# Five moves in the instruction order of a one-core attention and gated-expert kernel: first weights, key jobs, first softmax, output weights, bias

## Chip, core and metric

The kernel runs on one core of a Trainium2 chip. The core has a matrix engine (TensorE, PE in the profile; its weight loads stand apart as PEld), a vector engine (VectorE, DVE), a scalar engine (ScalarE, ACT), a slower general engine (GpSimd, POOL) and SyncE (SP), which issues nearly all DMAs. PE writes its results to PSUM, which this kernel uses as seven accumulators of 128 x 512 floats, `acc0` to `acc6`, and one more bank, `misc`. The metric is the device time of a launch in microseconds.

## What is computed

x has 2 x 2048 tokens of 2048 features. It is normalised, and two things are added to x: an attention of one head of width 512 and a low-rank expert layer of 64 experts of rank 8.

```python
xn = layernorm(x)
q, k, v = split(xn @ Wqkv + bqkv)
attn = softmax(q @ k.T / sqrt(512)) @ v @ Wo + bo
scores = (xn @ Wq_w.T) @ keys.T
gate = softmax of the 16 largest scores, 0 elsewhere
ffn = 2 * ((xn @ A_w.T) * gate, per expert) @ B_w.T
return x + attn + ffn
```

Everything is in 32-bit floats.

## The kernel before

**Numbers.** A float is split in two: `hi`, a copy in the reduced format `fp32r` that PE takes (`split_hi`, line 127, on ScalarE), and `lo`, what is left (`split_lo`, line 130, on VectorE). A product is three matmuls, lo x hi, hi x lo and hi x hi (`PASSES`, `product`, line 135). So each operand costs a ScalarE cast and a VectorE residue before PE can use it.

**Stages.** The 4096 tokens are 8 blocks of 512.

1. `first_block` (0 to some 70 us) makes value projections of block 0 out of rows of x: four row tiles of 128 tokens are loaded (`load`), their statistics taken (`normal`: `bn_stats` on VectorE, a power on POOL), scaled (`scale`), transposed on PE (`turn`, four groups of four) and split. Weights come in eight pieces: `piece()` loads one and casts it, `low(n)` makes its residue, on POOL for pieces 2 to 4, on VectorE for the others. `ps[t]` is the accumulator of row tile t. `turn` writes its groups into banks 0, 1, 2 and 0 again; `ps` takes banks 3 to 6.
2. Blocks 0 and 1 are projected plainly. The pairs of blocks (2,3), (4,5) and (6,7) are projected by a scheme of seven products in place of eight. Its phases are P1, P2, P6, P5, P3, P7, P4, each with six feature items and one value item `V` (first in P2 and P3, last in the others). An item takes 24 matmuls of 0.227 us, 5.4 us; a value item 96 shorter ones, 11.8 us. Weight pieces (`fetch`, tiles `pw`) are loaded two items ahead, cast and split. `beside` lists what each phase does next to its products, step by step, some steps behind each item: `split_steps` for the next phase's tokens, and in the last pair *key jobs* (`key_list`) and query sums (`query_steps`). A key job reads a quarter of a block's keys, makes the seven combinations for the scores and stores them: seven casts, seven residues and four sums of 128 x 256, two loads, four stores. In the last pair, P6 has jobs 0 to 2, P5 3 and 4, P7 5 and 6, and P4 job 7 with the loads (`ql`, `kl`) and splits (`qp`) of the first queries.
3. Scores. Four pairs of query blocks against eight key groups, seven products each: 224 steps g of six matmuls, 1.36 us (`score`, line 1170). Exact row maxima are kept (`greatest`, line 1134), gathered at the end of a block (`maxes`, lines 1210 to 1222) and spread over the partitions by a matmul (`spread`, line 1232). `side` holds, by step g, what is dealt beside: `keys`, `combos` (combinations of the output weights: four loads, four sums, lines 1344 to 1347, four stores), and the first softmax. `begin[0]` is step 65, the first at which weighted sums run between the scores.
4. `soft(c, part)` makes the softmax of one unit of 128 x 1024: part 0 subtracts the maximum (line 1252), part 1 takes the exponential (line 1256), part 2 casts, splits and adds to the sum (lines 127, 130, 1268). `weigh` multiplies with the values (line 135, `acc<-ph,vt`).
5. After the last score the weighted sums of blocks 6 and 7 run alone, c = 0 to 31, with the first loads of the output projection beside them; `load_bo(0)` loads the bias for half of the output columns. Then the output projection runs in seven products again (line 1464). `residual` loads a tile of x and adds the bias to it on POOL (line 1448).

**What sets the order.** The program is one list. Each engine works through its own instructions strictly in the order in which the build puts them; the build takes them by readiness and by place in the program, so that a load can stand far ahead of where it is written. `behind(...)` pins an instruction behind a given earlier one of the same engine. A DMA on SP waits, in its place, until its target is free or its source is written, and what is behind it on SP waits too.

Of the kernel before, what the change touches and what calls it, by code (L numbers as in the profile page):

```python
# [26 lines left out]
NT = T // P  # L27
# [35 lines left out]
def attn_ffn_kernel(ctx: ExitStack, tc, x, xT, wq, wv, wob, bqk, bv, bo, keysT, out):  # L63
# [36 lines left out]
    def acc(n=None):  # L100

        if n is None:
            n = banks.pop(0)
            banks.append(n)
        return psum.tile([P, T], F32, name="acc", tag=f"acc{n}", bufs=1)
# [230 lines left out]
    def first_block():  # L336


        xs0 = [r_xs, r_xs, r_xs] + [big(j) for j in range(16, 21)]
        xn = [r_xh([P, 2, T], FR, "xh") for c in range(NCH)]  # L340
        rows, mv = {}, const.tile([P, NT, 2], F32, name="mv", bufs=2)
        rs = const.tile([P, NT], F32, name="rs")
        nm = const.tile([P, NT], F32, name="nm")

        def load(t, cols):
            rows[t] = [xs0[2 * t + c]([P, 1024], F32, "xs") for c in range(2)]
            for c in range(2):
                for h in range(1024 // cols):
                    a = h * cols
                    (nc.scalar if t == 0 and c else nc.sync).dma_start(  # L350
                        rows[t][c][:, a : a + cols],
                        x[t * P : (t + 1) * P, c * 1024 + a : c * 1024 + a + cols],
                    )

        def normal(t):
            st = const.tile([P, 4, 6], F32, name="st6", bufs=2)
            row_stats(mv[:, t, :], rows[t], 0, st)
            last["nm"] = nc.vector.tensor_scalar(nm[:, t : t + 1], mv[:, t, 0:1], -1.0, None, ALU.mult)
            rstd(rs[:, t : t + 1], mv[:, t, 1:2], 1)

        def scale(t):
            for n in range(4):
                c, h = divmod(n, 2)
                v = rows[t][c][:, h * 512 : (h + 1) * 512]
                if n < 3:
                    last["row"] = nc.vector.tensor_scalar(
                        v, v, mv[:, t, 0:1], rs[:, t : t + 1], ALU.subtract, ALU.mult
                    )
                else:
                    nc.scalar.activation(v, v, AF.Identity, bias=nm[:, t : t + 1])  # L370
                    last["mul"] = nc.scalar.mul(v, v, rs[:, t : t + 1])

        def turn(t, g0=0, g1=NCH // 4):
            sl = slice(t * P, (t + 1) * P)
            for g in range(g0, g1):
                pt = acc(g % 3)
                for j in range(4):
                    c = 4 * g + j
                    k = (c % 8) * P
                    nc.tensor.transpose(pt[:, j * P : (j + 1) * P], rows[t][c // 8][:, k : k + P], ident)  # L380
                for part in range(2):
                    for j in range(4):
                        hi, lo = (xn[4 * g + j][:, a, sl] for a in range(2))
                        pj = pt[:, j * P : (j + 1) * P]
                        if part == 0:
                            split_hi(hi, pj)
                        else:
                            last["row"] = split_lo(lo, pj, hi)

        r_w0 = Ring(sb, "h0", "h1", "h2", "h3", "B25", "B26", "B32", "B33")  # L390

        def mul(ps, wh, t, c2):
            sl = slice(t * P, (t + 1) * P)
            for cc in range(2):
                c = 2 * c2 + cc
                product(
                    ps[:, :VH], lambda a: xn[c][:, a, sl], lambda b: wh[:, b, cc, :],
                    c == 0, c == NCH - 1,
                )

        N2 = NCH // 2
        warm = half(0)([P, T], mybir.dt.bfloat16, "warm")
        nc.vector.memset(warm, 0.0)
        pw = misc()
        for j in range(25):
            nc.tensor.matmul(pw, warm[:, :P], warm, start=True, stop=True)
        load(0, 512)
        normal(0)
        scale(0)

        wh = []

        def piece():
            wh.append(wv_hi(0, len(wh), r_w0))

        def low(n):
            with behind("row", "nm", "mul"):
                wh[n] = weights_lo(*wh[n], nc.gpsimd if 2 <= n < 5 else None)

        piece()  # L420
        piece()
        low(0)
        low(1)
        piece()
        turn(0, 0, 2)
        low(2)
        piece()
        turn(0, 2, 4)
        low(3)
        piece()  # L430
        low(4)
        load(1, 1024)
        ps = [acc(3 + t) for t in range(NT)]
        with behind("row"):
            normal(1)
        piece()
        low(5)
        load(2, 1024)
        for t in range(NT):
            for c2 in range(N2):  # L440
                if t + 1 < NT and c2 == 2:
                    scale(t + 1)
                    if t + 2 < NT:
                        with behind("row"):
                            normal(t + 2)
                if t == 0 and c2 == 4:
                    for n in range(6, N2):
                        piece()
                        low(n)
                    load(3, 1024)  # L450
                    constants()
                if t + 1 < NT and c2 == 6:
                    with behind("pe"):
                        turn(t + 1)
                mul(ps[t], wh[c2], t, c2)
        qr = router_in()
        for t in range(NT):
            with behind("row"):
                values_out(0, t, 0, r_ev, qr, ps[t])
        flush()  # L460
        ps = [acc(t) for t in range(NT)]
        banks[:] = 4, 5, 6, 0, 1, 2, 3
        for c2 in range(N2):
            w = wv_piece(1, c2)
            for t in range(NT):
                mul(ps[t], w, t, c2)
        for t in range(NT):
            values_out(0, t, 1, r_ev, qr, ps[t])
        return xn, qr
# [208 lines left out]
    def mixed(*lists):  # L678

        n = max(map(len, lists))  # L680
        return [
            st for k in range(n) for ls in lists
            for st in ls[k * len(ls) // n : (k + 1) * len(ls) // n]
        ]

    def beside(j, ph):
# [34 lines left out]
        if ph == "P3":  # L721
            if more:
                n = x_steps(j + 1, *b00)
                steps = mixed(split_steps(j, "P7", *b01), n[1][:2])
                return n[0], s1[-2:-1] + steps[:3] + s1[-1:] + steps[3:]
            q_ = query_steps(0, big(*GROUPS[3]), ((0, 1),))
            return [], q_[:1] + mixed(split_steps(j, "P7", *b01), q_[1:3]) + [lambda: None] + q_[3:]
        if ph == "P7":
            if more:
                n = x_steps(j + 1, *b10)  # L730
                return n[0], mixed(split_steps(j, "P4", *b10), n[1][:2])
            ks_ = key_list(5, 7)
            q_ = query_steps(1, big(*GROUPS[2]), ((0, 1),))
            return [], q_[:1] + mixed(split_steps(j, "P4", *b10), q_[1:3], ks_[:-6]) + ks_[-6:] + q_[3:]
        if more:
            return x_steps(j + 1, *b01)[0] + x_steps(j + 1, *b11)[0], mixed(
                x_steps(j + 1, *b00)[1][2:], split_steps(j + 1, "P1", *b00)[:2],
# [3 lines left out]
        kl = lambda i: lambda: key_load(i)  # L741
        k = key_list(7, 8, False)
        return [], [
            [ql(0), ql(1)], [qp(0), ql(2), *k[:2]], [qp(1), ql(3), *k[2:4]], [qp(2), ql(4), *k[4:6]],
            [qp(3), ql(5), *k[6:]], [qp(4), ql(6), kl(0), kl(1)], [kl(2), kl(3), qp(5), qp(6)],
        ]

    XU, YU, XV, YV = {}, {}, {}, {}
# [326 lines left out]
    n = 0  # L1075
# [475 lines left out]
        keys(n, g, g - 2)  # L1551
    spaced(NG1 + 36, query_steps(2, r_tp))
    spaced(2 * NG1 + 35, query_steps(3, r_tp))
    slots = [2 * NG1 + 45, 2 * NG1 + 50] + [3 * NG1 + k for k in (9, 17, 38, 44, 50, 56)]
    for k, g in enumerate(slots):
        spaced(g, combos(k // ND, k % ND))

# [13 lines left out]
                    deal(g, [loads[n]])  # L1571
                deal(g if n < 4 else g + 4, [splits[n]])
    deal(begin[0] - 8, [lambda c=c: load_v(c) for c in range(3)])
    deal(begin[0] - 3, [lambda c=c: soft(c) for c in range(2)])
    done = 0
    last["add"] = last["dve"]
    for g in range(begin[-1]):
# [45 lines left out]
    while done < NW * NPAIR:  # L1623
        weigh(done)
        done += 1
        c, d = divmod(done - NW * (NPAIR - 1), ND)
        if d == 0 and 1 <= c <= 18:

            k, part = (c - 1) // 2, (c - 1) % 2
            if part == 0:  # L1630
                if k < 8:
                    half_of[k] = moving(0, STEPS[k // 2], 2 * (k % 2))
                    with behind("sp"):
                        half_of[k][0]()
            elif k:
                half_of[k - 1][1]()
        if d == 0 and c == 18:
            load_bo(0)
        if d == 0 and c in (20, 24, 28):
            ahead(c // 4 - 5)  # L1640
# [75 lines left out]
```

## Time and profile before

| | |
|---|---|
| time, median of 3 runs | 2615.39 us (2614.67 to 2617.12) |
| profiled execution, its own time | 2614.46 us |
| span of its trace | 2612.3 us |
| mean granted PE clock | 0.998 |
| matmuls of line 1464, output projection | 609.4 us, x2688, 389 ns |
| matmuls of the pair phases, 128 x 512 | 694.0 us, x3024, 390 ns |
| adds of the bias on POOL, line 1448 | 234.4 us, x128, 1838 ns |
| packets of the 16 DMA engines | 608.08 MB, mean 233 GB/s |

A duration is that of one instruction from start to end; neighbours overlap, so 128 x 512 matmuls of 390 ns follow each other every 227 ns. Idle time is given with what ended it. Stretches and instructions are in us from the start of the span; "x4" is four instructions put in one row, and what stands in square brackets is the idle time just before the row and who ended it.

### The profile page before, as it was taken

The numbers are of one execution on the slowest core, as the hardware profiler recorded it, in microseconds if no ns is written. First come the engines' busy times: TensorE is split into PE (matmuls) and PEld (weight loads), VectorE is DVE, ScalarE is ACT, GpSimd is POOL, SyncE is SP. The second block draws the span as 40 slices with busy tenths as digits, with TensorE's granted clock in tenths as the row PEclk, the third lists the DMA queues.
The fourth block names the chain that finished last, engine by engine and source line by source line (L and its number), as shares of the span: only waits on it lengthen the run. The fifth ranks groups of instructions, "written<-read, shape, count | busy, mean of one in ns | idle before, by whom it ended". The sixth has DMA issues, their size and how long they took to land. (4 is left out here: it accounts for less than half of the span.)

```text
span 2612.3 us, 34449 instructions
## 1 busy us (share of the span) xinstructions
PE 2588.7 (99%) x12690; PEld 2187.4 (84%) x12690; DVE 1910.3 (73%) x2688; ACT 925.1 (35%) x1377; POOL 548.2 (21%) x318
## 2 busy tenths in 40 slices
PE   8999999999999999999999999999999999999999
PEld 8889888888888888888887888878877888888887
DVE  6557639867878677776768869688698776787675
ACT  4333323323332233343445546354364222332221
POOL 2311420001000010000000000000032655576654
PEclk9999999999999999999999999999999999999999
DMA  6667775668436684577999798788898545565552
GB/s 236 241 245 259 280 268 188 207 215 278 158 129 225 220 275 130 170 259 244 314 323 317 243 338 282 270 317 282 276 325 289 170 156 164 188 213 181 170 166 101
DMA packets 326649, 608.08 MB, mean 233 GB/s; under 512 B 27672, under 2 KB 150608, under 8 KB 326480
## 3 DMA queue, kind: packets, MB, share of 16 engines
q1 hardware_dynamic: 313520, 575.99, 65.0%
q10 hardware_dynamic: 12960, 29.89, 3.4%
q8 instruction: 100, 1.64, 0.3%
q14 instruction: 69, 0.57, 0.1%
HBM read 450.42 MB, written 155.35 MB: 232 GB/s over the span
## 5 line engine op out<-in xcount | busy, mean ns | idle before, releaser
L135 PE MATMUL acc<-t,pw 128*128 128x512 f32 x3024 | 694.0, 390 | 3.7 <-DVE pw L130 3.7
L135 PEld LDWEIGHTS acc<-t,pw 128*128 128x128 f32 x3024 | 565.3, 188 | 121.9 <-DVE pw L130 4.1
L1464 PE MATMUL acc<-wb,s 128*128 128x512 f32 x2688 | 609.4, 389 | 0.0
L1464 PEld LDWEIGHTS acc<-wb,s 128*128 128x128 f32 x2688 | 504.5, 188 | 104.8
L1448 POOL TENSOR_TENSOR xo<-xo,bo_bc 128x512 f32<-128x512 f32 x128 | 234.4, 1838 | 868.8 <-DMA bo_bc<-in_bo 593.0
L135 PE MATMUL acc<-ph,vt 128*128 128x512 f32 x1536 | 380.0, 392 | 4.2 <-DVE ph L130 2.4
L135 PEld LDWEIGHTS acc<-ph,vt 128*128 128x128 f32 x1536 | 289.0, 189 | 67.7 <-DVE ph L130 3.5
L1170 PE MATMUL acc<-qt,kt 128*128 128x512 f32 x1344 | 334.2, 391 | 1.1 <-DVE qt L130 1.0
L1170 PEld LDWEIGHTS acc<-qt,kt 128*128 128x128 f32 x1344 | 252.2, 188 | 56.8 <-DVE qt L130 2.2
L127 ACT CAST pw<-pw 128x1024 fp32r<-128x1024 f32 (+1 forms) x168 | 177.7, 1058 | 343.3 <-PE acc L135 236.1
L130 DVE TENSOR_TENSOR pw<-pw 128x1024 fp32r<-128x1024 f32 (+1 forms) x168 | 213.4, 1270 | 70.9 <-ACT pw L127 69.5
L135 PE MATMUL acc<-xh,wh 128*128 128x512 f32 x1152 | 263.6, 390 | 0.0
L135 PEld LDWEIGHTS acc<-xh,wh 128*128 128x128 f32 x1152 | 215.6, 188 | 44.9
L127 ACT CAST s<-xz 128x1024 fp32r<-128x1024 f32 x112 | 118.0, 1055 | 376.3 <-PE acc L1464 314.2
L135 PEld LDWEIGHTS acc<-pw,t 128*128 128x128 f32 x2016 | 245.7, 188 | 2.0 <-DVE yv L790 0.8
L135 PE MATMUL acc<-pw,t 128*128 128x264 f32 x2016 | 246.4, 283 | 0.6 <-DVE yv L790 0.6
L130 DVE TENSOR_TENSOR s<-xz,s 128x1024 fp32r<-128x1024 f32 x112 | 170.7, 1526 | 45.3 <-ACT s L127 45.3
L130 DVE TENSOR_TENSOR wh<-wu,wh 128x512 fp32r<-128x512 f32 x96 | 82.0, 870 | 97.6 <-ACT wh L127 97.4
L544 POOL TENSOR_TENSOR zt<-zt,g 128x512 f32<-128x512 f32 x24 | 39.9, 1672 | 504.3 <-DMA g<-gd 275.7
L1453 DVE TENSOR_TENSOR xo<-xo,acc 128x512 f32<-128x512 f32 x128 | 86.8, 680 | 52.7 <-POOL xo L1494 24.1
L127 ACT CAST t<-xq 128x1024 fp32r<-128x1024 f32 x84 | 88.3, 1051 | 98.2 <-PE acc L135 41.3
L130 DVE TENSOR_TENSOR t<-xq,t 128x1024 fp32r<-128x1024 f32 x84 | 106.2, 1269 | 22.1 <-ACT t L127 21.6
(166 smaller groups left out, 2488.1 us busy)
## 6 DMA issues: line engine op xcount, KB each, us to landing
vt<-v_d SPq DMA_DIRECT2D x128, 512.0 KB, 5.8
kt<-kp_d SPq DMA_DIRECT2D x224, 256.0 KB, 5.9
pw<-sq_d SPq DMA_DIRECT2D x72, 512.0 KB, 4.2
xo<-in_x SPq DMA_DIRECT2D x128, 256.0 KB, 3.3
xz<-oz_d SPq DMA_DIRECT2D x64, 512.0 KB, 4.6
out_y<-xo SPq DMA_DIRECT2D x128, 256.0 KB, 2.5
pw<-in_wq SPq DMA_DIRECT2D x54, 512.0 KB, 4.3
wu<-in_wq SPq DMA_DIRECT2D x48, 512.0 KB, 6.1
```

The costliest lines, as they stand in the source:

```text
L127: return nc.scalar.copy(hi, src)
L130: return (eng or nc.vector).tensor_tensor(lo, src, raw(hi), ALU.subtract)
L135: last["pe"] = nc.tensor.matmul(ps, st(a_), mv(b_), start=first and n == 0, stop=end and n == 2)
L544: nc.gpsimd.tensor_tensor(zt, zt, gx[n], ALU.mult)
L1170: last["pe"] = nc.tensor.matmul(ps, st[:, d, a, :], mv[c][:, d, :], start=not more and d == 0 and i == 0, stop=d == 1 and i == 2, skip_gro ...
L1448: nc.gpsimd.tensor_tensor(xs, xs, bo_bc[q // (NB // 2 * NH), c], ALU.add)
L1453: nc.vector.tensor_tensor(xs, xs, ps, op)
L1464: nc.tensor.matmul(ps, st[a_][:, kk, sl], mv[b_], start=not more and kk == 0 and n == 0, stop=kk == ND - 1 and n == 2, skip_group_check=more,)
```

## The change

- In `turn` the four groups go to banks 0, 1, 2 and 6. `ps` is no longer taken at once: the accumulator of row tile t is taken when its products begin.
- Pieces 5, 6 and 7 are loaded and cast right behind row tile 1, ahead of row tile 2; the residue of piece 5 comes ahead of the statistics of row tile 1.
- In the last pair, job 5 goes from P7 to P3; the query sums' stores in P7 come ahead of the last five key steps. In P4 the splits of the first queries come one item later, and the steps of key job 7 are grouped 3, 2, 3.
- The `combos` slots of the last quarter go from 9, 17, 38, 44, 50, 56 to 7, 14, 21, 38, 44, 50.
- The first softmax unit is dealt in three parts at steps 60, 61 and 62, the second half of it at 63; before, both at 62 and 63.
- `load_bo(0)` is written at c = 28 in place of c = 18.

```diff
-                pt = acc(g % 3)
+                pt = acc((0, 1, 2, 6)[g])
...
         load(1, 1024)
-        ps = [acc(3 + t) for t in range(NT)]
+        for n in range(5, N2):
+            piece()
+        low(5)
         with behind("row"):
             normal(1)
-        piece()
-        low(5)
         load(2, 1024)
+        ps = []
         for t in range(NT):
+            ps.append(acc(3 + t))
             for c2 in range(N2):
...
                 if t == 0 and c2 == 4:
-                    for n in range(6, N2):
-                        piece()
-                        low(n)
+                    low(6)
+                    low(7)
                     load(3, 1024)
                     constants()
...
             q_ = query_steps(0, big(*GROUPS[3]), ((0, 1),))
-            return [], q_[:1] + mixed(split_steps(j, "P7", *b01), q_[1:3]) + [lambda: None] + q_[3:]
+            ks_ = key_list(5, 6)
+            return [], q_[:1] + mixed(split_steps(j, "P7", *b01), q_[1:3], ks_[:-5]) + q_[3:] + ks_[-5:]
...
-            ks_ = key_list(5, 7)
+            ks_ = key_list(6, 7)
             q_ = query_steps(1, big(*GROUPS[2]), ((0, 1),))
-            return [], q_[:1] + mixed(split_steps(j, "P4", *b10), q_[1:3], ks_[:-6]) + ks_[-6:] + q_[3:]
+            return [], q_[:1] + mixed(split_steps(j, "P4", *b10), q_[1:3], ks_[:-5]) + q_[3:] + ks_[-5:]
...
-            [ql(0), ql(1)], [qp(0), ql(2), *k[:2]], [qp(1), ql(3), *k[2:4]], [qp(2), ql(4), *k[4:6]],
-            [qp(3), ql(5), *k[6:]], [qp(4), ql(6), kl(0), kl(1)], [kl(2), kl(3), qp(5), qp(6)],
+            [ql(0), ql(1)], [ql(2), *k[:3]], [qp(0), ql(3), *k[3:5]], [qp(1), ql(4), *k[5:]],
+            [qp(2), qp(3), ql(5)], [qp(4), ql(6), kl(0), kl(1)], [kl(2), kl(3), qp(5), qp(6)],
...
-    slots = [2 * NG1 + 45, 2 * NG1 + 50] + [3 * NG1 + k for k in (9, 17, 38, 44, 50, 56)]
+    slots = [2 * NG1 + 45, 2 * NG1 + 50] + [3 * NG1 + k for k in (7, 14, 21, 38, 44, 50)]
...
-    deal(begin[0] - 3, [lambda c=c: soft(c) for c in range(2)])
+    deal(begin[0] - 5, [lambda c=c: soft(0, c) for c in range(3)])
+    deal(begin[0] - 2, [lambda: soft(1)])
...
-        if d == 0 and c == 18:
+        if d == 0 and c == 28:
             load_bo(0)
```

## The prediction

> **What bounds the kernel.** I read the page's engine shares first, then the list of who waited for whom, cut to TensorE (PE), then the table by stretches around each hole, and last the order of time inside it.
>
> ```profile
> span 2612.3 us, 34449 instructions
> PE 2588.7 (99%) x12690; PEld 2187.4 (84%) x12690; DVE 1910.3 (73%) x2688; ACT 925.1 (35%) x1377; POOL 548.2 (21%) x318
> ```
>
> ```profile
> PE acc L135 <- DVE wh L130: 3.8, 1, 3.8
> PE acc L135 <- DVE pw L130: 3.7, 1, 3.7
> PE misc L1232 <- DVE mq L1222: 2.5, 3, 1.2
> PE acc L135 <- DVE ph L130: 2.4, 1, 2.4
> ...
> PE acc L135 <- ACT ph L127: 1.2, 1, 1.2
> ```
>
> The waits are us in total, times, longest. PE idles 2612.3 - 2588.7 = 23.6 us, in a few holes. No matmul is added or removed, so the change is worth only what it does to holes and to the half-clock stretches behind them. Distances between matmul starts put the holes at 15.9 to 19.7 us (first weights), 1290.2 to 1294.1 (last phase, P4, of the last pair), 1412.8 to 1415.1 (first softmax), 1899.4 to 1900.6 (last maxima) and 1988.9 to 1991.5 (end of the weighted sum). Each edit touches one of them.
>
> ```profile
> 1288.89:1292.30 3.41, 1.48 (x7) 1.00 1.01 394
> 1292.30:1295.71 3.41, 1.63 (x7) 1.00 0.90 363
> 1411.77:1415.18 3.41, 1.57 (x7) 1.00 0.95 303
> 1415.18:1418.59 3.41, 3.41 (x8) 0.50 0.27 92
> ...
> 1988.62:1992.03 3.41, 1.00 (x5) 1.00 0.63 186
> 1992.03:1995.44 3.41, 3.41 (x9) 0.50 0.45 161
> ```
>
> The columns are the stretch, its length, PE busy, granted clock, DMA share, GB/s. Twice here, and again at 19.13 to 22.54, PE ran for 3.41 us at half clock, which costs up to 3.41 / 2 = 1.7 us. **Row against rule.** The Trainium skill, "TensorE: Matmul & The Clock Gate" ("HAM oscillation"), puts the limit at idle gaps of over about 3.4 us. In this trace holes of 0.65 and 1.19 us together, and one of 2.6, were followed by half clock, while the hole of 3.9 us, split over two windows with 1.48 and 1.63 busy, was not. The rows fit a count of work per window: 1.00 busy, or 1.57 of which 0.47 is one matmul of only 48 rows, is too little; 1.48 of full ones is enough. By the rule, closing the 1413 and 1990 holes would save the holes alone; by the row 1.7 us more each, 3.4 in all. I take the row.
>
> **1. First weights.** Nothing is added. Pieces 6 and 7 (2 x 270 KB) now go ahead of row tile 2 (1 MB) on SP, which then lands about 0.54 MB / 0.37 MB per us = 1.5 us later; its statistics ran at 21.5, behind work that ends no earlier than 20.6 (below), so that is hidden.
>
> ```profile
> 15.23 0.88 DVE L130 TENSOR_TENSOR xh<-acc,xh 128x128 fp32r<-128x128 f32 x4 [1.68 <-ACT xh L127]
> 16.03 2.46 DVE L206 BATCH_NORM_STATS2 st<-xs 128x6 f32<-128x512 f32 x4
> ```
>
> VectorE (DVE) sets this stage. Four banks for the transposes take away its 1.68 us wait, so its first residues end near 14.3 instead of 16.1. Then comes the residue of piece 5 (0.70, from 14.5, when ScalarE has cast it), then the statistics (2.46 + 0.27 + 0.2, to 18.2), then POOL's power (0.96), which the piece used to hide and which now lies bare. Scaling of row tile 1 starts near 19.2 instead of 20.1. PE does piece 5 at about 15.5 to 16.2 and then waits for the transposes of that tile, at 19.8 instead of 20.97: the hole moves, and the slow window stays. Gain 1.1. Against it: bank 6 is also the accumulator of row tile 3, whose first matmul must now wait for the sixteenth residue of its own transposes. In the old trace these ran 38.4 (first transpose) to 43.1 (last residue), with 16 x 0.11 + 12 x 0.12 = 3.2 us of PE work to cover 4.7: 1.5 lost, where PE ran on before. Net loss 0.4 (from 2 gained to 3.3 lost, if that hole also brings a slow window).
>
> **2. Key jobs.** One job (7 casts of 0.41 on ScalarE; 7 residues and 4 sums of 0.42 on DVE = 4.6 us; 2 loads and 4 stores on SP) goes from P7 to P3. DVE was busy 8.88 and 8.21 of 10 us in 1204 to 1224 (P3), and 9.70 and 8.16 in 1254 to 1274 (P7). Also the query splits of P4 come an item later.
>
> ```profile
> 1284.78 0.80 SPq L631 DMA_DIRECT2D pw<-in_wq  x1
> ...
> 1290.22 1.04 ACT L127 CAST qt<-qt 128x1024 fp32r<-128x1024 f32 x1 [3.28 <-DMA qt<-qs_d]
> 1291.72 1.04 ACT L127 CAST pw<-pw 128x1024 fp32r<-128x1024 f32 x1 [0.46 <-DMA pw<-in_wq]
> ```
>
> The weight piece was issued only at 1284.78: on SP it stands behind the value stores of P7 (1277.5 to 1283.5), which wait for a DVE that was late with key steps. It landed 6.9 us later, in a stretch with the DMA at 0.95 to 1.03. With 4.6 us less on DVE I put the stores 3.5 us earlier, so the piece near 1281.3, landing 1288.2, cast 1289.3, residue 1290.5, no longer behind a query cast: needed at 1290.2, hole 0.3 to 0.5. Gain 3.4 (nothing if only ScalarE's order changes, since the landing alone explains 1291.64; 3.9 at most; a loss is the second rival).
>
> **3. First softmax.** The subtraction stood at 1411.52 on DVE, behind both sums (1409.11 and 1409.92). Dealt two steps earlier it follows the first: 1409.8, exponential 1411.2, cast 1412.3 to 1413.0 instead of 1414.47 to 1415.09. PE's 1.19 us and 0.13 for the residue go. The 0.65 before the maxima product stays, since the same DVE work is ahead of it; it is what is late next. With 1.2 more busy the window keeps full clock: 1.7. Gain 3.0 (0 to 3.6).
>
> **4. Output weights.** The eighth combination job leaves slot 56 of the last quarter. Its four sums (0.69 each) at 1891.73, 1892.94, 1894.56 and 1897.04 stood inside the chain of the last maxima, whose end at 1900.48 held PE 1.38 us. Gain 1.4 (0 to 1.5). The other slots move by up to three steps: the load at 175 may wait on SP for stores of `ot` (landed about 1758), some 2 us ahead of key loads that are issued eight steps (11 us) early. Hidden; DVE at 3.62 and 5.46 of 10 in 1810 to 1830 takes the job at 189.
>
> **5. The bias.**
>
> ```profile
> 1988.75 2.15 POOL L1448 TENSOR_TENSOR xo<-xo,bo_bc 128x512 f32<-128x512 f32 x1 [0.66 <-DVE L L1268]
> 1989.70 1.75 DVE L130 TENSOR_TENSOR ph<-sp,ph 128x512 fp32r<-128x512 f32 x1
> ```
>
> Five POOL adds in 1971 to 1991 each lengthen one DVE operation by 1.1 us (0.68 to 1.79, 1.22 to 2.31), 5.4 in all, and PE waits 2.57 for the last residue. Whether the edit moves an add is not sure: the load of the bias stands at 1902.43 in the trace, far ahead of its place in the program (near 1956), so the build orders it by readiness. But the DMAs of the eighth combination leave SP between 1886 and 1898, where token loads may go instead, and part 4 frees DVE time. I take one add less before the last residue: 1.1 + 1.7 (busy 2.1 in that window) = 2.8, between 0 and 2.6 + 1.7 = 4.3.
>
> **Sum.** +0.4 - 3.4 - 3.0 - 1.4 - 2.8 = -10.2 on the profiled execution's 2614.46 (span plus 2.2): 2604.3. The median of the three runs is 0.9 above it: 2605.2.
>
> **Rivals.** *Half of it*: the DMA still sets the landing of the P4 piece and the bias moves nothing, the case in which two parts don't do what they say. +0.4 - 3.0 - 1.4 = -4.0: 2611.4. For it: DMA at 0.95 and the bias at 1902. Against: SP's queue is visibly late.
>
> *Slower*: the key job in P3.
>
> ```profile
> ACT kst L127 <- DMA kp_d<-kst: 33.4, 19, 5.1
> ```
>
> ScalarE waited 19 times for a key store to land, 1.8 us on average, 5.1 at most, with weight casts queued behind it. P3's fifth item has 1.4 us of slack (residue ends 1217.4, needed about 1218.8). Each of the four new stores can cost 5.1 - 1.4 = 3.7; from the third on it eats the whole gain. Four: 14.8, and two slow windows 3.4, so 18.2 - 10.2 = 8.0 lost: 2623.4. Against it: the average wait is near the slack, and P5 carries two jobs with no hole.
>
> *All of it*: 1.1 without the bank wait, 3.9, 3.0, 1.4, 4.3, and the small waits at 1951 and 1964 (0.6 + 0.3): -14.6, 2600.8.
>
> **Chances.** Forecast 0.50, half 0.22, slower 0.13, all 0.15. A measurement of this kernel can tell about 0.2% (5.2 us) from no change. Faster: 0.50 + 0.15 + 0.03 of the half case = 0.68; the rest of that case and a little of the third make no change 0.20, slower 0.12. Range 2600.0 to 2617.5: it takes in the first, the half and the full case and part of the slower one.
>
> **What would show it.** Half clock gone after 1415 and 1992, still there near 19 to 23; PE waiting near 41 us for a residue of `xh`; the P4 piece issued on SP by about 1281 and no PE wait on `pw`; no wait of 1.2 us before the last `mq` product; fewer lengthened DVE operations before the last `ph`. It is wrong if a PE wait on `pw` appears in P3 or P7, or if the bank wait at 41 us brings a slow window.

## The result and the profile after

The changed kernel takes 2608.03 us (median of 8 runs, 2605.63 to 2610.36) against 2615.89 us for the kernel before (8 runs, 2611.67 to 2619.87). The ratio is 0.9971, 95% interval 0.9960 to 0.9982, so 7.9 us are gained (4.7 to 10.5). The forecast was 2605.2, in a range of 2600.0 to 2617.5. The total was near. What it is made of was not: of its five steps one came out at its place in the size worked out and one roughly, two brought nothing at their place, one had its gain by way of another edit, and an amount of 3.3 us was in no sum.

First the page of the changed kernel, then its list of who PE waited for (us in total, times, longest):

```profile
span 2608.6 us, 34456 instructions
PE 2587.2 (99%) x12690; PEld 2186.9 (84%) x12690; DVE 1910.3 (73%) x2688; ACT 924.8 (35%) x1377; POOL 520.0 (20%) x318
```

```profile
PE acc L135 <- DVE xh L130: 3.7, 3, 1.5
PE acc L380 <- DVE xs L366: 3.2, 2, 3.0
...
PE acc L1172 <- ACT sp L1182: 1.5, 1, 1.5
```

PE idles 2608.6 - 2587.2 = 21.4 us where it idled 23.6. The waits of 3.7 for `pw`, of 3.8 for `wh` and of 2.4 for `ph` are gone or small. In their place stand 3.0 for the scaled row tile (`xs`), 1.4 for the bank of row tile 3 (one of the three waits for `xh`; the longest of them, 1.5, is for residues of row tile 1), 1.5 for ScalarE's copy of `sp`, and (not copied here) 1.8 for `yv`, in a part of the kernel that no edit touches. (From line 433 on, line numbers of the changed kernel are one to three higher than before.)

This profiled execution is the slowest of its eight, 2610.36 us, only 4.1 below the profiled one of before, while the medians differ by 7.9. Two profiles alone would mislead here, and the reason for it is the main finding. The same stretches as in the prediction (length, PE, PEld, DVE, ACT and POOL busy, granted clock, DMA share, GB/s), of the changed kernel:

```profile
1291.24:1294.66 3.42, 3.42 (x16) 2.82 (x15) 0.83 (x3) 0.57 (x2) 0.00 (x0) 1.00 1.03 311
1410.83:1414.25 3.42, 1.88 (x8) 0.84 (x6) 3.36 (x8) 2.05 (x3) 0.00 (x0) 1.00 1.03 335
1414.25:1417.66 3.41, 3.41 (x9) 2.73 (x9) 2.43 (x4) 2.28 (x5) 0.00 (x0) 0.50 0.05 17
```

The hole at 1290 is closed: PE is busy throughout, as it is from 1987 to 1994 (3.40 of 3.40 us in two stretches), in the place of the hole at the end of the weighted sum. The one at 1413 is not closed, and half clock follows it as before.

### The profile page after: what moved, and what is told of

Same layout as the page of the kernel before. It is cut to its first block, busy times and chain, and to the rows that moved or that the text cites. A ratio compares the mean times of both kernels' runs of the same rounds, so it can differ in the third digit from the quotient of the medians.

```text
span 2608.6 us, 34456 instructions
## 1 busy us (share of the span) xinstructions
PE 2587.2 (99%) x12690; PEld 2186.9 (84%) x12690; DVE 1910.3 (73%) x2688; ACT 924.8 (35%) x1377; POOL 520.0 (20%) x318
## 5 line engine op out<-in xcount | busy, mean ns | idle before, releaser
L1450 POOL TENSOR_TENSOR xo<-xo,bo_bc 128x512 f32<-128x512 f32 x128 | 207.4, 1627 | 893.2 <-DMA bo_bc<-in_bo 588.8
```

What stands on the lines that cost most here:

```text
L1450: nc.gpsimd.tensor_tensor(xs, xs, bo_bc[q // (NB // 2 * NH), c], ALU.add)
```

## The experiments

Each kernel was run beside the kernel before; a ratio is to that, with its 95% interval, and 0.1% is 2.6 us. Every run also reports its mean granted clock, to three digits. One minus it, times the span, is the time that half clock can cost, half of what its stretches last (it costs less where PE would wait anyway); its mean over many runs tells more than one profile. For the kernel before it is 0.9971 over 91 runs, 7.6 us.

**The five edits one by one.** The first takes only the first weights:

```diff
-                pt = acc(g % 3)
+                pt = acc((0, 1, 2, 6)[g])
...
-        piece()
-        low(5)
...
+        ps = []
```

> The kernel before with the first edit alone (banks 0, 1, 2, 6 for the transposes, pieces 5 to 7 ahead of row tile 2, residue of piece 5 ahead of the statistics). Theory 'by the trace after': this edit is a loss of about 2 us: PE stands for row tile 3's first product (1.4 us, bank 6), has nothing of row tile 0 left to put beside the transposes, and keeps its hole of 3 us at 17 to 20. Time 2616 to 2619, +0.05 to +0.15%. Theory 'by the prediction': +0.4 us, so nothing that can be told, and the stage ends near where it did. Rival 'window': if the loss seen in the profile is only another phase of the half-clock window, the stage ends within 0.5 us of before's (event at 82 us).

Measured: 0.9998 (0.9989 to 1.0006), nothing that can be told. The first stage ends when PE starts its first 128 x 512 product. With this edit that is at 72.80, 71.75 (the changed kernel, two profiles) and 71.33 us (this run), mean 72.0; in eight profiles without the edit it is at 70.70 to 72.02, mean 71.1. The ranges overlap, so a cost of some 0.8 us is an estimate from few profiles; it lies between the two theories.

The reverse, the changed kernel with this edit undone:

> The changed kernel with the first edit undone. By the trace after: 2 us faster than the changed kernel, near 2606, 0.9963 of before. By the prediction: 0.4 us faster, 0.997. If edit 1 had gained at its place (-1.1 without the bank wait): slower than the changed kernel by 1 us, 0.9975.

Measured: 0.9964 (0.9951 to 0.9976), in the direction of the first theory, but the interval holds the changed kernel's 0.9971 too, and at its very end the 0.9975 of a gain at its place. The time does not decide.

The slots of the combination jobs alone (`slots`, last quarter: 7, 14, 21, 38, 44, 50):

> The kernel before with the new slots of the combination jobs alone; the bias load stays written at c = 18. By the trace after: the freed places on SP around 1890 take four token loads and the bias, four POOL adds run before 1912, the hole at 1990 and the half clock behind it go (-4.3), the 1.4 us before the last maxima go but a wait of 1.5 us for a tile comes at 1892: -4 us in all, 2612. By the prediction (parts 4 and 5 gain each at its own place): -1.4, hole at 1990 still there with the load of the bias left where it was: 2614.5.

Measured: 0.9984 (0.9977 to 0.9990), -4.2 us, as the first theory has it. The bias load is left where it was written, and yet the hole at 1990 is gone. POOL's timeline (start, us) of this run shows why:

```profile
1907.17 6.66 POOL L1448 TENSOR_TENSOR xo<-xo,bo_bc 128x512 f32<-128x512 f32 x4 [591.17 <-DMA bo_bc<-in_bo]
```

PE ran without a wait through the place of the hole:

```profile
1974.66 23.28 PE L135 MATMUL acc<-ph,vt 128*128 128x512 f32 x102
```

Four adds now run in a row at 1907, in 1.7 us each. In the profile of before only one stood there, and took 21.35 us:

```profile
1907.63 21.35 POOL L1448 TENSOR_TENSOR xo<-xo,bo_bc 128x512 f32<-128x512 f32 x1 [593.01 <-DMA bo_bc<-in_bo]
```

Five others stood at 1971 to 1991 beside the last weighted sums; in this run two are left there, from 1983.34 on, and PE does not wait. What moved the others are token loads on SP, where the eighth combination's four loads and four stores used to stand; SP's queue in the changed kernel:

```profile
1885.86 0.45 SPq L1449 DMA_DIRECT2D xo<-in_x  x1
1888.11 3.04 SPq L1284 DMA_DIRECT2D vt<-v_d  x2
```

Two more token loads follow at 1892.54 and a fourth at 1901.92, and the bias between them at 1898.57, earlier than the 1902.43 of before, although its edit writes it later.

The bias edit alone (`c == 18` to `c == 28`):

> The kernel before with the bias load written at c = 28 alone. By the trace after: this edit is inert once the slots are changed; alone it holds the bias, and so all adds, until behind the value loads of about 1960, so the adds stay beside the last weighted sums or come to stand behind them: 0 (-1.5 to +1.5), 2615.9, the hole at 1990 still there. By the prediction: one add less before the last residue and no half clock, -2.8: 2613. Rival 'late bias frees the end': no add at all before the last residue: -4.3, 2611.6.

Measured: 0.9995 (0.9987 to 1.0003), no change that can be told; the prediction's 0.9989 lies within the interval as well. The profile decides for the first theory: the bias is loaded at 1963.76, six adds run from 1969 to 1990, and PE's waits for `ph` are 0.76, 0.79 and 1.56, 3.1 us in all where before had one of 2.41. In the changed kernel the edit makes no difference at all: built with `c == 18` it has the same instructions in the same order on every engine.

The key jobs alone:

```diff
+            ks_ = key_list(5, 6)
...
-            ks_ = key_list(5, 7)
+            ks_ = key_list(6, 7)
...
-            [ql(0), ql(1)], [qp(0), ql(2), *k[:2]], [qp(1), ql(3), *k[2:4]], [qp(2), ql(4), *k[4:6]],
-            [qp(3), ql(5), *k[6:]], [qp(4), ql(6), kl(0), kl(1)], [kl(2), kl(3), qp(5), qp(6)],
+            [ql(0), ql(1)], [ql(2), *k[:3]], [qp(0), ql(3), *k[3:5]], [qp(1), ql(4), *k[5:]],
+            [qp(2), qp(3), ql(5)], [qp(4), ql(6), kl(0), kl(1)], [kl(2), kl(3), qp(5), qp(6)],
```

> The kernel before with the second edit alone (key job 5 in P3, splits of the first queries an item later). Theory 'hole and half clock': the hole of 3.9 us at 1294 shrinks to under 1 us; the hole alone is worth 3.1, and in three of four profiles of kernels that keep it a half clock of one or two stretches of 3.41 us came with it, so some 1.7 us more on average: -4.8 us, ratio 0.9982. Theory of the prediction: 3.4 us and no half clock, 0.9987. Rival 'key store holds ScalarE': PE waits on pw in P3 (1140 to 1225), and the gain is under 1 us.

Measured: 0.9973 (0.9963 to 0.9984), -7.1 us, more than any of the three, and nearly all that the whole change brings. The mean granted clock of its 7 runs is 0.9986, against 0.9972 of the 19 of before beside them: 3.7 of the 7.1 us are half clock. PE ran without a wait from 1283.63 to 1296.26, through the place of the hole, and its waits for a `pw` piece are 0.90 and 0.20 us, both in the value item of P4. SP's queue in this run says how:

```profile
1272.72 0.81 SPq L631 DMA_DIRECT2D pw<-in_wq  x1
1277.22 1.80 SPq L169 DMA_DIRECT2D v_d<-vs  x2
```

The late piece, issued at 1284.78 before, is now issued at 1272.72, ahead of the value stores instead of behind them. The stores themselves hardly came earlier: the first at 1277.22 here and at 1277.47 before, while PE is 1.1 us earlier in this place than before. The job moved from P7 to P3, with the new lists of these two phases, does this: in the program built with the new list of P4 alone, SP's piece loads and value stores keep the order of before.

The softmax in parts alone (`soft(0, c)` from step 60 and `soft(1)` at 63):

> The kernel before with the first softmax dealt in parts, alone. By the trace after: the earlier subtraction pushes the last sum of scores behind it, ScalarE's copy of the accumulator comes behind the exponential, and PE waits 1.5 us there in place of 1.2 before the weighted sum: 0 (-0.5 to +0.5), ratio 1.000, half clock near 1415 in the profile about as before. By the prediction: -3.0, 0.9989, no hole of over 0.7 us at 1412 to 1416 and full clock behind it.

Measured: 0.9992 (0.9984 to 1.0000), -2.1 us. The prediction's 0.9989 lies within the interval and no gain is its upper end, so the time does not decide. The profiles show what became of the waits. What the distances between PE's matmul starts exceed their usual 0.227 us by, from 1398 to 1418 and without half clock, is 3.6 to 3.8 us in four profiles without this edit (before, bias alone, keys alone, and the kernel below) and 3.5 to 3.8 in four with it (this one, the changed kernel twice, and the changed kernel without the first weights). The waits did not go. VectorE, ScalarE and PE in the changed kernel:

```profile
1410.03 1.23 DVE L1254 TENSOR_TENSOR sp<-sp,mbc 128x1024 f32<-128x1024 f32 x1
...
1412.18 0.69 DVE L1179 TENSOR_TENSOR sp<-sp,acc 128x512 f32<-128x512 f32 x1
```

```profile
1411.29 1.06 ACT L1258 ACTIVATE sp<-sp 128x1024 f32<-128x1024 f32 x1 [2.43 <-DVE sp L1254]
1412.26 0.57 ACT L1182 COPY sp<-acc 128x512 f32<-128x512 f32 x1
```

```profile
1412.96 0.93 PE L1172 MATMUL acc<-qt,kt 128*128 128x512 f32 x3 [1.54 <-ACT sp L1182]
```

The subtraction starts at 1410.03, but the sum of scores (line 1179) now stands behind it, at 1412.18 where it was at 1409.92, and ScalarE's copy of an accumulator stands behind the exponential. That copy frees the bank that the next score product writes: PE waits 1.54 us there.

**Both doubtful edits undone**, parts 2, 4 and 5 kept:

> The changed kernel with the first weights and the first softmax undone: parts 2, 4 and 5 alone. By the trace after: both are worth nothing, so it is as fast as the kernel without the first weights alone, 0.9964. By the prediction: slower than the changed kernel by 3.0 - 0.4 = 2.6 us, 0.9981.

Measured: 0.9958 (0.9944 to 0.9971), so not the loss of 2.6 us that the prediction's steps would give; and beside the 0.9964 with the first weights alone undone, undoing the softmax as well cost nothing that can be told.

**The bank.** The changed kernel with `acc((0, 1, 2, 6 if t < 3 else 0)[g])`:

> The changed kernel, but the fourth group of row tile 3 goes to bank 0 instead of 6, so row tile 3's accumulator doesn't wait for the residue of its own transposes. Theory 'bank wait': PE's wait of 1.4 us at 43.5 goes, -1.4 us against the changed kernel, 0.9966. Theory 'VectorE is the limit': the first product of row tile 3 starts earlier, but its later ones wait for the same residues, so under 0.4 us: 0.9970. A loss is open too: the fourth group of tile 3 then waits for bank 0's first residues (+0.5).

Measured: 0.9963 (0.9951 to 0.9975). The changed kernel's wait and this one's PE in the same place:

```profile
43.50 3.67 PE L135 MATMUL acc<-wh,xh 128*128 128x264 f32 x28 [1.38 <-DVE xh L130]
```

```profile
40.13 6.09 PE L135 MATMUL acc<-wh,xh 128*128 128x264 f32 x48
```

The wait goes, nothing comes in its place, and the stage ends at 69.78 us, 2.0 before the faster of the changed kernel's two profiles. No half clock fell into this stage here, so up to 1.7 of that is not the bank's; in the time alone, 1.4 us are too little to be told.

**Half clock.** In the profiles of four kernels that keep the hole at 1290, half clock came behind it, though not in the profile of before. With PE busy 0.26 (first weights alone), 0.90 (output weights), 1.23 (bias) and 0.81 us (softmax) in the stretch ahead of it, it lasted one stretch of 3.41 us in three of them and two in the bias-alone run. That run:

```profile
1289.32:1292.73 3.41, 1.23 (x6) 0.69 (x4) 0.46 (x1) 2.06 (x2) 0.00 (x0) 1.00 1.03 408
1292.73:1296.14 3.41, 2.59 (x6) 2.10 (x7) 3.41 (x6) 2.10 (x2) 0.00 (x0) 0.50 0.63 253
1296.14:1299.56 3.42, 3.42 (x9) 2.65 (x9) 2.85 (x4) 1.45 (x2) 0.00 (x0) 0.50 0.95 273
```

So the kernel before was run with idle products in the hole, and nothing else:

```diff
+                    if ph == "P4" and j == PAIRS[-1] and m == 3:
+                        for _ in range(12):
+                            with behind("pe"):
+                                nc.tensor.matmul(
+                                    ps, ops[0][0][:, 0, :P], ops[0][0][:, 0, :], start=True, stop=True
+                                )
```

> The kernel before, with twelve idle products of 0.227 us (2.7 us; their result is overwritten by the first real product) put ahead of item 3 of the last phase P4, where PE waits 2.8 to 3.9 us for the weight piece. Nothing of the change is in it, and the wait itself stays. Theory 'half clock': most of what the key jobs alone gained beyond their hole of 3 us was the half clock that the hole sets off, so this alone gains 2 to 4 us, ratio 0.9985 to 0.9992, and the mean granted clock of the runs rises from 0.9971 to about 0.998; full clock after 1294 in the profile. Theory 'only the hole counts' (that of the prediction, where this hole set off no half clock): 0, ratio 1.000, clock unchanged; a loss of 0.2 us if the fillers outlast a short hole.

Measured: 0.9989 (0.9983 to 0.9995), -2.9 us, with no wait removed. The mean granted clock of its 21 runs is 0.9983, against 0.9970 of the 30 of before beside them: 4.5 us of half clock in place of 7.8, so 3.3 less, and the rest of the time is the same within 0.4. The idle products ran from 1291.28 to 1294.16, PE then waited 0.84 for the piece; the stretch of the hole and the one behind it:

```profile
1291.87:1295.28 3.41, 2.57 (x12) 1.83 (x11) 1.56 (x2) 2.17 (x3) 0.00 (x0) 1.00 1.02 401
1295.28:1298.70 3.42, 3.42 (x16) 2.81 (x16) 3.42 (x6) 2.33 (x3) 0.00 (x0) 1.00 0.64 246
```

The same filling for the hole at 16 to 19.6 us, in the kernel with parts 2, 4 and 5:

```diff
+                if t == 0 and c2 == 5:
+                    for _ in range(24):
+                        with behind("pe"):
+                            nc.tensor.matmul(
+                                pw[:, :VH], xn[0][:, 0, :P], wh[0][:, 0, 0, :], start=True, stop=True
+                            )
```

> Parts 2, 4 and 5 alone (first weights and first softmax undone), with 24 idle products of 128 x 264 (0.11 us each, 2.6 us) put where PE waits 3.5 us for the residue of piece 5 of the first weights. Theory 'half clock': full clock at 20 to 23 us, where PE's transposes and products otherwise run at half speed: 1 to 1.7 us faster than the same kernel without them, 0.9953. Theory 'VectorE sets this stage': what PE does faster there waits for VectorE's next residues all the same, under 0.4 us: 0.9958.

Measured: 0.9973 (0.9964 to 0.9982), slower than either theory has it, and no gain over the 0.9958 (0.9944 to 0.9971) of the same kernel without them. The twelve transposes take 1.57 us in place of 2.71 in its profile, and then PE waits:

```profile
23.91 2.29 PE L135 MATMUL acc<-wh,xh 128*128 128x264 f32 x14 [1.79 <-DVE xh L130]
```

VectorE sets this stage in this profile, and the full clock there goes into a wait for it; the stage ends at 70.53, where 70.70 was. It is one profile: in that of the last kernel below, filled in the same way, half clock came at 25.51 all the same and the stage ends at 72.56.

**The changed kernel again**, on the chip of the last runs:

> The changed kernel as it is, beside the others on the same chip. By the first comparison: 0.9971, mean granted clock 0.9992, one or two stretches of half clock in the profile.

Measured: 0.9967 (0.9955 to 0.9980), clock 0.9988.

**The last combination job**, two steps earlier (36, 42, 48), on the kernel with the filled start:

> As the filled start, and the last three combination jobs at steps 36, 42 and 48 of the last quarter in place of 38, 44 and 50, so that the last sums end ahead of the transposition that begins the maxima of block 6. Theory 'sums in the chain': the waits of 1.3 us at 1892 and of 1.0 us at 1901 before the mq products go, -2.3 us against the filled start, 0.9944. Rival 'store of tw_d': VectorE waits for the store of the last job before it can write ls, wherever the sums stand, and 0.7 of the 1.3 stays: -1.6. Rival 'subtractions': the last chain is held by three subtractions of 1.2 us between its small steps, and the wait at 1901 stays: -1.3.

Measured: 0.9954 (0.9941 to 0.9968), median 2604.19 us, beside 2608.74 for the filled start and 2608.87 for the changed kernel on the same chip. The changed kernel's VectorE, in the maxima of block 6:

```profile
1882.98 0.71 DVE L1212 STREAM_TRANSPOSE mt<-M 128x512 f32<-128x512 f32 x1
1883.61 0.65 DVE L1348 TENSOR_TENSOR tp<-tp 128x512 f32<-128x512 f32 x1
...
1888.99 0.69 DVE L130 TENSOR_TENSOR ls<-L,ls 128x512 fp32r<-128x512 f32 x1 [0.72 <-DMA tw_d<-tp]
```

The sums had left the chain of block 7 and stood in that of block 6, and a residue that had to wait for the job's store came between as well. PE waited at both `mq` products:

```profile
1891.95 0.50 PE L1234 MATMUL misc<-mq,onesr 48*128 48x512 f32 x1 [1.16 <-DVE mq L1224]
1901.43 0.46 PE L1234 MATMUL misc<-mq,onesr 48*128 48x512 f32 x1 [0.82 <-DVE mq L1224]
```

With the jobs two steps earlier, PE waits at neither of the two:

```profile
1887.87 0.50 PE L1239 MATMUL misc<-mq,onesr 48*128 48x512 f32 x1
1888.30 3.67 PE L135 MATMUL acc<-ph,vt 128*128 128x512 f32 x15
1891.89 0.50 PE L1239 MATMUL misc<-mq,onesr 48*128 48x512 f32 x1
```

Both rivals fall: neither the residue of `ls` nor the subtractions hold a product here. In time it is 4.5 us less than the filled start (the intervals just overlap), more than the 2.3 of the theory; 1.7 of it is half clock by the mean clocks (0.9987 and 0.9993). This is the fastest kernel tried; against the changed one its interval still overlaps.

## Why the prediction came out near, and where its steps failed

**Key jobs, -3.4: right at its place, and short of a term.** The wait of 3.71 went, 0.6 came at 1316: -3.1. The route was another than I gave, so the size is in part luck: I let the stores come 3.5 us earlier; the build put the piece ahead of them. The step that failed is in the row against the rule: "the hole of 3.9 us, split over two windows with 1.48 and 1.63 busy, was not" followed by half clock, and so I gave this hole none. The stretches of 3.41 us run free of the program: in the profile of before, half clock begins at 19.13, 1415.18 and 1992.03, whole multiples of 3.413 us apart (409 and 169), and in other executions of nearly the same program at other phases (25.02 in the changed kernel, 1.73 stretches behind 19.13). (The Trainium skill, "TensorE: Matmul & The Clock Gate", Part 1, says so of the first warming up; here it holds in the middle of a kernel.) That the hole fell evenly over two was the chance of one execution; in four other profiles it fell mostly into one. The filled hole measures it: 3.3 us on average (3.7 by the clocks of the keys alone), the largest single term of the result. That a count of work decides was borne out (at this hole 0.26 to 1.23 busy gave half clock; 1.48, 1.63 and 2.57 did not), but PE busy is a rough measure of it: 1.60 and 1.88 gave half clock elsewhere (last section). Preferring the row to the rule of the Trainium skill (the same page, "HAM oscillation"), idle gaps over about 3.4 us, was right: waits of 2.68 and 3.01 us were enough in two of the four profiles, and of 1.81 and 2.20 near 394 in two others. What was wrong was to read a chance as a fact.

**First weights, +0.4: right in mechanism, somewhat off in size.** The wait for bank 6 is there (1.38 forecast as 1.5), scaling of row tile 1 starts at 19.40 (forecast 19.2), the hole stays and moves to the transposes (3.0). The stage ends some 0.8 later by few profiles, where 0.4 was forecast.

**First softmax, -3.0: failed.** The step is "Dealt two steps earlier it follows the first" sum, with "the same DVE work" ahead of the maxima product. The subtraction took the place of the second sum, which carries a bank release through ScalarE. I had moved one instruction earlier and not asked who was pushed back: the waits of 0.65 and 1.19 gave way to one of 1.54. The half clock there is chance as well: it stands in two of the five profiles with the edit and in five of the nine without it.

**Output weights, -1.4: failed at its place, and gained elsewhere.** The forecast took the sums out of one chain and did not look where slot 50 puts them: into the chain before it. The waits at 1892 and 1901 together are 0.8 more than before. The gain of the edit, 4.2 alone, comes from the places on SP that it frees.

**Bias, -2.8: the effect is right, its cause the one named as uncertain.** The hole at 1990, 2.41 us of wait, went because "token loads may go instead" and the adds with them. The edit on the bias does nothing. The half clock behind this hole was chance again: it stands in two of the five profiles that keep the hole (before and first weights; not bias, keys and softmax), so the 1.7 for it was too much as an average; with the output weights alone, half clock fell by 1.3 us in all.

Taken together: in the mean over runs the half clock fell from 7.6 us to 2.4 (13 runs), 5.2 of the 7.9. The sum had 3.4 of its 10.2 from half clock and 6.8 from holes; 5.2 and some 2.7 came. Too little of the one and too much of the other nearly cancelled: that the total came near was luck. The rivals fell: no wait on `pw` appeared in P3, and the load of the P4 piece did move. One sign of being wrong did show, if small: PE waited 0.69 and 0.19 us for a `pw` piece in P7 in two profiles of kernels with the key edit, though in neither of the changed kernel's own.

Left open: the five edits alone sum to 15 us, the whole brings 7.9. The intervals, 1.7 to 2.7 us to each side for each edit, are part of it. Another part may be waits in stages that no edit touches and that come and go between executions of one kernel: the two profiles of the changed kernel show 1.80 us and none for `yv` near 564, and none and 0.56 for `pw` at 394, where other kernels have up to 2.20. What sets them was not tried. Nor is any kernel shown to beat the changed one beyond its interval.

## What to carry to other kernels

Where PE idles for some 2 us or more, price the hole and the half clock it may set off, as an average over where it can fall, not as one profile shows it; mean granted clocks of many runs give that price, and idle products in the hole test it. When an instruction is moved ahead on an engine, name the one that it passes and who waits for that. An edit that leaves a queue can be worth more by what takes its place than at its own spot.

## What the runs showed of the hardware that was not expected

A stretch at half clock with PE busy 2.59 of 3.41 us was followed by a second one, while one at full clock with 1.48 was not followed by any. Counted as work the two agree. Count each matmul with the distance at which its kind follow each other at full clock in these traces (0.227 us for 512 columns, 0.121 for 264, 0.109 for a transpose), whatever the clock, and only the part that falls into the stretch:

| kernel, start of the stretch | clock | PE busy, us | work, us | clock of the next |
|---|---|---|---|---|
| bias alone, 1289.32 | full | 1.23 | 1.07 | half |
| bias alone, 1292.73 | half | 2.59 | 1.28 | half |
| last kernel, 394.15 | full | 1.60 | 1.32 | half |
| changed, 21.61 | full | 1.88 | 1.34 | half |
| before, 1288.89 | full | 1.48 | 1.32 | full |
| before, 19.13 | half | 2.83 | 1.41 | full |
| before, 1292.30 | full | 1.63 | 1.49 | full |

In the fourteen profiles, the 33 stretches ahead of half clock hold at most 1.40 us of work by this count, and the 10,594 others at least 1.32; seven lie between and go either way. PE busy separates them less well, because a matmul that stands alone counts there with its 0.39 us. This is an estimate from starts of matmuls, and it was not used to predict anything here.

How long an add on POOL takes varies widely: the one at 1907 took 21.35 us in the profile of before and 1.69 with the first weights alone, in the same place of the order, and four in a row took 1.7 us each at nearly the same time in the changed order. Beside the long one VectorE ran without a pause, and only its operation at 1927.74, near the add's end, was lengthened (1.78 us where its like take 0.68). That VectorE held the add is a reading of this; no run tests it.
